# Turned aggregations of a four-layer graph network: 64x128 matmuls on two row halves of TensorE instead of 64x64 matmuls on four quadrants

## The chip, the cores and the metric

The kernel runs on one core of a Trainium2 chip. The metric is the device time of one execution in microseconds. Three runs of the kernel before gave 2742.39, 2743.45 and 2743.74 us; the median is 2743.45 us. One further execution was taken by the hardware profiler; it took 2741.53 us, and all views of the profile come from it. In those views PE is TensorE (matmuls), PEld is its weight loads, DVE is VectorE, ACT is ScalarE, POOL is GpSimd and SP is the engine that issues most transfers.

## The reference

128 graphs of 64 nodes with 512 features go through four layers. Each layer mixes the nodes of a graph with some 64x64 matrix and the features with dense weights, adds the result to its input and normalises it:

```
x = LN(x + HypergraphConv_2(LN(relu(HypergraphConv_1(x, adj))), adj) + x)   # 512 -> 1024 -> 512
x = LN(x + scaled_attention(x) @ x @ w)                                     # 64x64 matrix per graph
x = LN(x + gcn3(relu(gcn2(relu(gcn1(x))))))                                 # each: adj @ (h @ W) + b
x = LN(x + heads(softmax(q k^T) + adj + exp(-adj)) @ v @ Wout + bout)       # 8 heads of 64
```

Everything is float32. What matters here are the products of a 64x64 matrix of one graph (adj, or a matrix made from it) with that graph's 64 rows of features: `mat^T @ x`, 64x64 by 64x512.

## The kernel before

**Tiling.** Two graphs make a pair of 128 rows (128 partitions: rows 0 to 63 are one graph, rows 64 to 127 the other). Four pairs make a group of 512 rows, and 16 groups are worked through. Within a group the dense weights are applied to all 512 rows at once, and the mixing of nodes is done graph by graph.

**Dense products.** `multiply` (L546) does a 512x512 by 512x512 product with seven block products instead of eight; `product` (L528) issues the matmuls of one block product, each with a stationary operand of 128x128 and a moving one of 128x256 (L539). The first group uses plain products instead (`rows_of`, L897).

**Aggregations that come out turned.** The dense product that follows an aggregation needs its left operand with features on the partitions. So the aggregation is done with the features as the stationary operand and the graph's matrix as the moving one: the result is features by nodes, already turned. `graph_T` (L470) does this for one duo, that is two pairs or four graphs: for four chunks `c` of 128 features, two pairs `p`, two halves `f` of a chunk, and two graphs `g` of the pair, one matmul (L481) with 64 rows (the nodes of graph `g`) by 64 columns of weights (half a chunk of features) and 64 moving columns. Graph `g` sits on rows 0 to 63 or 64 to 127 of the array, half `f` on columns 0 to 63 or 64 to 127, so four matmuls in a row use the four quadrants. The results of graph `g` go to the PSUM tile `ps[g]`, whose partitions 0 to 63 and 64 to 127 are the two halves of a chunk. When the 32 matmuls are done, each of the two tiles is copied to SBUF in one instruction (ACT at L492, or DVE for the second one at L490 where `both` is set).

`graph_T` is called ten times for a group: twice for layer 0 (tiles `gt_l`, L755 or L932), four times for its hidden features (tiles `gt_l0h`, L801 or L977), twice in layer 1 (L853, or L1037 and L1064) and twice in layer 2 (L1079). `second_half` has the same loop written out for the second step of layer 2 (L1115 to L1125, tiles `gth`), where `f` and the row half `h` choose the quadrant; ACT then takes each result through a relu (L1130).

**Other small matmuls**, which stay as they are: the 64x64 matmuls on diagonal quadrants in `prepare` (`sps`, L692, and `dps`, L707, whose moving operand has one column), the attention's scores and outputs (`dot` L1326, `pv` L1385), the last aggregation of layer 2 (`agg`, L1156, 64x64 weights, 512 moving columns), and transposes with a stationary operand of 64 rows by 128 columns and 64 moving columns of an identity, on the two row halves (`xtp` L1176, `ptp` L1361).

**What orders the work.** The lists `start`, `order`, `step_1` and `step_last` (L1402 to L1422) interleave three groups: the first half of one, the second half of the group before and the tail of the one before that. The generators yield between steps, and between such points a scheduler chooses the order of each engine's instructions; `behind` (L501) holds instructions back behind a named one. PSUM has four buffers in `ps_gt` (the aggregations' results among others) and four in `ps_acc` (dense products). Weights come by DMA through a ring of 20 tiles.

Of the kernel before, what the change touches and what calls it, by code (L numbers as in the profile page):

```python
# [14 lines left out]
P = 128  # L15
C = 64
# [25 lines left out]
def kernel(  # L42
# [88 lines left out]
    ten, vec, act = Engine(nc.tensor, PE), Engine(nc.vector, DVE), Engine(nc.scalar, ACT)  # L131
# [338 lines left out]
    def graph_T(src, mat, dst, duo, key, both=False):  # L470

        ps = [ps_gt.tile([P, 4, 2, C], FP, name=f"gt_{key}_{duo}_{g}", tag="gt") for g in range(2)]
        for c in range(4):
            for p in range(2):
                for f in range(2):
                    for g in range(2):
                        rows, c0 = slice(g * C, (g + 1) * C), c * P + f * C  # L480
                        ten.matmul(  # L481
                            ps[g][f * C : (f + 1) * C, c, p, :],
                            src(2 * duo + p)[rows, c0 : c0 + C],
                            mat[rows, 2 * duo + p, :],
                            start=True, stop=True,
                        )
        o = dst[:, :, duo * Q : (duo + 1) * Q].rearrange("p c (a g i) -> p c a g i", a=2, g=2)
        for g in range(2):
            if both and g == 1:
                vec.tensor_copy(o[:, :, :, g, :], ps[g])  # L490
            else:
                act.copy(o[:, :, :, g, :], ps[g])  # L492
# [256 lines left out]
    def first_half(g):  # L749
# [4 lines left out]
        for duo in range(2):  # L754
            graph_T(pair, g["sm"], left.t, duo, f"l0_{q}")  # L755
# [42 lines left out]
        for duo in range(2):  # L798
            for u in range(2):
                with behind("l2b_0.p3") if q == 1 else nullcontext():  # L800
                    graph_T(  # L801
                        lambda p: h[p // 2][:, p % 2, u * D : (u + 1) * D], g["sm"], lefts[u].t, duo, f"l0h{u}_{q}"
                    )
            if duo == 0:
                if q == 1:
                    constant(g)
                yield "c2a"
# [43 lines left out]
        for duo in range(2):  # L851
            with behind("agg_0.p") if q == 1 else nullcontext():
                graph_T(pair, t, left.t, duo, f"l1_{q}", both=True)  # L853
# [219 lines left out]
    def second_half(g):  # L1073
# [28 lines left out]
        g2 = big.tile([P, G, D], FP, name=f"g2_{q}", tag="big")  # L1102
# [12 lines left out]
        for c2 in range(2):  # L1115
            ps = [ps_gt.tile([P, 2, G, C], FP, name=f"gth2_{q}_{c2}_{h}", tag="gt") for h in range(2)]
            for c in range(2):
                for p in range(G):
                    for f in range(2):
                        for h in range(2):  # L1120
                            rows, c0 = slice(h * C, (h + 1) * C), (2 * c2 + c) * P + f * C
                            ten.matmul(  # L1122
                                ps[h][f * C : (f + 1) * C, c, p, :],
                                g2[rows, p, c0 : c0 + C], g["atc"][rows, p, :], start=True, stop=True,
                            )  # L1125
            for c in range(2):
                k = 2 * c2 + c
                o = h2.t[:, k, :].rearrange("p (d h t) -> p d h t", d=2, h=2)
                for h in range(2):
                    act.activation(  # L1130
                        o[:, :, h, :], ps[h][:, c].rearrange("p (d a) i -> p d (a i)", d=2),
                        AF.Relu, bias=gb2_col[:, k : k + 1],
                    )
# [14 lines left out]
        for duo in range(2):  # L1148

            pool, tag = (ps_acc, "acc") if q == 0 else (ps_gt, "gt")  # L1150
            ps = [pool.tile([P, D], FP, name=f"agg_{q}_{duo}_{p}", tag=tag) for p in range(2)]
            for h in range(2):
                for p in range(2):
                    rows = slice(p * C, (p + 1) * C)
                    mat = g["atc"][rows, 2 * duo + p, :] if p == h else g["atx"][rows, duo, :]
# [13 lines left out]
        for duo in range(2):  # L1169
            ps = [ps_gt.tile([P, KD, 2, C], FP, name=f"xtp_{q}_{duo}_{h}", tag="gt") for h in range(2)]  # L1170
            for c in range(KD):
                for p in range(2):
                    for h in range(2):
                        rows = slice(h * C, (h + 1) * C)
# [39 lines left out]
        ps = attend(g, 1, pts[1], v)  # L1214
# [159 lines left out]
    def attend(g, duo, pts, v):  # L1374

        q = g["q"]

        ps = [ps_acc.tile([P, 4, 2, C], FP, name=f"pv_{q}_{duo}_{gg}", tag="acc") for gg in range(2)]
        for hc in range(4):
            for p in range(2):  # L1380
                for h2 in range(2):
                    hd = 2 * hc + h2
                    for gg in range(2):
                        rows = slice(gg * C, (gg + 1) * C)
                        ten.matmul(  # L1385
                            ps[gg][h2 * C : (h2 + 1) * C, hc, p, :],
                            v[rows, 2 * duo + p, hd * C : (hd + 1) * C],
                            pts[p][rows, h2 * 4 + hc, :],
                            start=True,
                            stop=True,  # L1390
                        )
        return ps
# [9 lines left out]
    start = """  # L1402
# [175 lines left out]
```

## Time and profile before

| what | value |
|---|---|
| runs | 2742.39, 2743.45, 2743.74 us |
| profiled execution | 2741.53 us, its span 2739.8 us |
| PE busy | 2720.2 us |
| PE weight loads busy | 2348.2 us |
| DVE busy | 2079.1 us |
| ACT busy | 804.2 us |
| POOL busy | 38.0 us |
| mean traffic of the transfers | 148 GB/s |

A span runs from the first to the last instruction; the execution holds 1.73 us more around it. A float32 matmul shows as two pairs of a weight load and a matmul, so a group's count is twice that of the code's matmuls. Each record has a start and a duration; a matmul's duration covers its way through the array, so records overlap, and the distance from one start to the next on the same part of the array tells the pace better than a duration does. In lists of groups the fields are: line, engine, operation, output and inputs by name, then for TensorE rows*columns of the weights and the shape of the operand, the count, busy time in us, mean ns of one, and the idle time before.

### The profile page before, as it was taken

Reading aid. Unit: us, or ns where it says so; the run is one execution under the profiler, and the core shown is the slowest. Engines: PE = TensorE matmul, PEld = TensorE weight load, DVE = VectorE, ACT = ScalarE, POOL = GpSimd, SP = SyncE. Lnnn points to the kernel's source line nnn. Section 1 sums busy time; section 2 is a strip of 40 time slices with the busy share of each in tenths; the row PEclk is TensorE's granted clock in tenths of the full one; section 3 lists DMA queues with packets and bytes.
Section 4 is the critical chain, followed back from the end, with each engine's and each line's share of the span. In section 5 each row is a group of like instructions: output and inputs, shape, how many; then the busy total and the mean of one; then the engine's idle time right before and its main releaser. Section 6 shows DMA issues by size and latency. Waiting matters only on the chain.

```text
span 2739.8 us, 67717 instructions
## 1 busy us (share of the span) xinstructions
PE 2720.2 (99%) x28770; PEld 2348.2 (86%) x28770; DVE 2079.1 (76%) x4119; ACT 804.2 (29%) x1442; POOL 38.0 (1%) x71
## 2 busy tenths in 40 slices
PE   9999999999999999999999999999999999999998
PEld 8878888888888888888888888888888888888887
DVE  6877687876877778787786877778777687776866
ACT  3323323232232332322223232232323323232232
POOL 2000000000000000000000000000000000000000
PEclk9999999999999999999999999999999999999999
DMA  8534454454544545445454454545545455454541
GB/s 263 180 120 153 121 174 141 141 166 131 171 132 139 166 129 169 132 143 169 132 166 130 144 164 131 166 126 153 159 131 171 130 161 146 132 164 131 151 126 60
DMA packets 309388, 405.14 MB, mean 148 GB/s; under 512 B 57408, under 2 KB 185184, under 8 KB 309088
## 3 DMA queue, kind: packets, MB, share of 16 engines
q1 hardware_dynamic: 304256, 385.58, 47.4%
q0 software_dynamic: 4832, 15.24, 1.5%
q8 instruction: 228, 3.74, 0.6%
q14 instruction: 72, 0.59, 0.1%
HBM read 369.78 MB, written 30.93 MB: 146 GB/s over the span
## 4 chain that ended last, share of the span: by engine, by line
PE 95%; DVE 3%; ACT 1%; issue 0%; DMA 0%; POOL 0%; DVEq 0%; POOLq 0%
PE a_l0w L539 15%; PE b_l0w L539 7%; PE a_l2b L539 4%; PE a_q L539 4%; PE a_k L539 4%; PE a_l2a L539 4%; PE a_v L539 4%; PE c_l0w L539 4%; PE a_l1w L539 4%; PE a_wo L539 4%; PE a_l2c L539 4%; PE gt_l L481 3%; PE gt_l0h L481 2%; PE b_l1w L539 2%; PE b_l2a L539 2%; PE b_l2b L539 2%
## 5 line engine op out<-in xcount | busy, mean ns | idle before, releaser
L539 PE MATMUL a_l0w<-w2w,aT_l0h 128*128 128x256 f32 x720 | 164.3, 381 | 0.0
L457 DVE BATCH_NORM_STATS2 st_l<-x 128x6 f32<-128x512 f32 x244 | 157.7, 673 | 0.6
L539 PEld LDWEIGHTS a_l0w<-w2w,aT_l0h 128*128 128x128 f32 x720 | 135.6, 190 | 18.8
L463 DVE TENSOR_SCALAR x<-x,mv_l,rs_l 128x512 f32<-128x512 f32 x244 | 119.3, 542 | 2.2
L539 PE MATMUL b_l0w<-w2w,s_l0h 128*128 128x256 f32 x480 | 108.5, 379 | 0.0
L779 ACT ACTIVATE h<-h 128x1024 f32<-128x1024 f32 (+1 forms) x58 | 54.9, 947 | 178.5 <-DVE h L598 157.5
L539 PEld LDWEIGHTS b_l0w<-w2w,s_l0h 128*128 128x128 f32 x480 | 91.1, 190 | 12.5
L1130 ACT ACTIVATE aT_h<-gth,gb_col 128x256 f32<-128x256 f32 x128 | 48.5, 492 | 159.0 <-PE gth L1122 159.0
L447 ACT ACTIVATE rs_l<-mv_l,eps_t 128x4 f32<-128x4 f32 (+1 forms) x64 | 19.0, 297 | 257.0 <-DVE mv_l L458 245.3
L555 DVE TENSOR_TENSOR u_l0w<-a_l0w,b_bc 128x512 f32<-128x512 f32 x56 | 38.6, 690 | 69.2 <-PE a_l0w L539 69.2
L492 ACT COPY aT_l<-gt_l 128x512 f32<-128x512 f32 x146 | 77.1, 596 | 45.7 <-PE gt_l L481 45.7
L539 PE MATMUL a_l1w<-ww,aT_l 128*128 128x256 f32 x360 | 85.7, 381 | 2.1 <-issue 2.1
L539 PE MATMUL a_l2b<-gwbw,aT_h 128*128 128x256 f32 x360 | 86.6, 383 | 0.7 <-ACT aT_oT L1397 0.7
L539 PE MATMUL a_l2c<-gwcw,aT_h 128*128 128x256 f32 x360 | 86.3, 382 | 0.0
L539 PE MATMUL a_q<-aT_xT,wqw 128*128 128x256 f32 x360 | 85.1, 379 | 0.7 <-ACT aT_xT L1181 0.7
L539 PE MATMUL a_l2a<-aT_l,gwaw 128*128 128x256 f32 x360 | 85.0, 379 | 0.0
L539 PE MATMUL a_k<-aT_xT,wkw 128*128 128x256 f32 x360 | 85.0, 379 | 0.0
L539 PE MATMUL a_l0w<-w1aw,aT_l 128*128 128x256 f32 x336 | 80.8, 383 | 0.0
L539 PE MATMUL a_v<-wvw,aT_xT 128*128 128x256 f32 x336 | 80.8, 383 | 0.0
L539 PE MATMUL a_wo<-wow,aT_oT 128*128 128x256 f32 x336 | 79.5, 379 | 0.0
L539 PE MATMUL a_l0w<-w1bw,aT_l 128*128 128x256 f32 x336 | 79.4, 379 | 0.0
L539 PEld LDWEIGHTS a_l1w<-ww,aT_l 128*128 128x128 f32 x360 | 68.5, 190 | 11.6 <-issue 2.3
(528 smaller groups left out, 6488.4 us busy)
## 6 DMA issues: line engine op xcount, KB each, us to landing
w2w<-w2k SPq DMA_DIRECT2D x210, 256.0 KB, 2.6
x<-in_x_dram SPq DMA_DIRECT2D x15, 1024.0 KB, 5.7
w1aw<-w1ak SPq DMA_DIRECT2D x60, 256.0 KB, 2.6
w1bw<-w1bk SPq DMA_DIRECT2D x60, 256.0 KB, 2.7
ww<-wk SPq DMA_DIRECT2D x60, 256.0 KB, 2.8
gwaw<-gwak SPq DMA_DIRECT2D x60, 256.0 KB, 3.1
gwbw<-gwbk SPq DMA_DIRECT2D x60, 256.0 KB, 2.7
gwcw<-gwck SPq DMA_DIRECT2D x60, 256.0 KB, 2.7
```

The source lines that it names most:

```text
L447: act.activation(rs[:, at], mv[:, at, 1], AF.Sqrt, bias=eps_t)
L457: vec.bn_stats(st, xg[:, p, :])
L463: vec.tensor_scalar(xg[:, p, :], xg[:, p, :], mv[:, p, 0:1], rs[:, p : p + 1], ALU.subtract, ALU.mult)
L481: ten.matmul(ps[g][f * C : (f + 1) * C, c, p, :], src(2 * duo + p)[rows, c0 : c0 + C], mat[rows, 2 * duo + p, :], start=True, stop=True,)
L492: act.copy(o[:, :, :, g, :], ps[g])
L539: ten.matmul(acc[:, blk, :], lhsT, rhs, start=(first and blk == 0 and i == 0), stop=(last and i == n_k - 1), skip_group_check=True,)
L555: last_add[f"{key}.{what}"] = (act.copy(t, ps) if res is None else vec.tensor_add(t, ps, res(m, n))).ins
L779: act.activation(hn, hn, AF.Relu)
L1130: act.activation(o[:, :, h, :], ps[h][:, c].rearrange("p (d a) i -> p d (a i)", d=2), AF.Relu, bias=gb2_col[:, k : k + 1],)
```

## The change

Both loops lose the index over halves of a chunk. One matmul takes the whole chunk of 128 features as its weights, so it uses 64 rows by 128 columns of the array, and the two graphs of a pair stand on the two row halves. Moving operand, PSUM tiles, their layout and the copies out of them stay. The diff is whole:

```
@@ graph_T
         for c in range(4):
             for p in range(2):
-                for f in range(2):
-                    for g in range(2):
-                        rows, c0 = slice(g * C, (g + 1) * C), c * P + f * C
-                        ten.matmul(
-                            ps[g][f * C : (f + 1) * C, c, p, :],
-                            src(2 * duo + p)[rows, c0 : c0 + C],
-                            mat[rows, 2 * duo + p, :],
-                            start=True, stop=True,
-                        )
+                for g in range(2):
+                    rows = slice(g * C, (g + 1) * C)
+                    ten.matmul(
+                        ps[g][:, c, p, :], src(2 * duo + p)[rows, c * P : (c + 1) * P],
+                        mat[rows, 2 * duo + p, :], start=True, stop=True,
+                    )
@@ second_half
             for c in range(2):
                 for p in range(G):
-                    for f in range(2):
-                        for h in range(2):
-                            rows, c0 = slice(h * C, (h + 1) * C), (2 * c2 + c) * P + f * C
-                            ten.matmul(
-                                ps[h][f * C : (f + 1) * C, c, p, :],
-                                g2[rows, p, c0 : c0 + C], g["atc"][rows, p, :], start=True, stop=True,
-                            )
+                    for h in range(2):
+                        rows, c0 = slice(h * C, (h + 1) * C), (2 * c2 + c) * P
+                        ten.matmul(
+                            ps[h][:, c, p, :], g2[rows, p, c0 : c0 + P], g["atc"][rows, p, :],
+                            start=True, stop=True,
+                        )
```

In the compiled program PE has 11825 matmuls instead of 14897: 6144 matmuls of 64x64 have become 3072 of 64x128. They stand at the same places between the same other matmuls, and no other engine has an instruction more or less.

## The prediction, made before the changed kernel ran

> **What bounds the kernel now.** I read the page from the top: busy times, the clock's row of slices, the chain that ended last.
>
> ```profile
> PE 2720.2 (99%) x28770; PEld 2348.2 (86%) x28770; DVE 2079.1 (76%) x4119; ACT 804.2 (29%) x1442; POOL 38.0 (1%) x71
> ...
> PEclk9999999999999999999999999999999999999999
> ...
> PE 95%; DVE 3%; ACT 1%; issue 0%; DMA 0%; POOL 0%; DVEq 0%; POOLq 0%
> ```
>
> TensorE is busy in 2720.2 of 2739.8 us and carries 95% of the chain; the clock is granted in full throughout. Only 19.6 us of the span are idle on PE. So what the matmuls of an aggregation take longer or shorter is given to the end nearly one to one. Next, the chain in a stretch that holds two aggregations, and the groups of TensorE by shape:
>
> ```profile
> 1146.94 2.02 PE gt_l0h L481 x128
> 1148.96 1.92 PE c_l2b L539 x8
> ```
>
> ```profile
> L481 PE MATMUL gt_l0h<-smat,h 64*64 64x64 f32 x3840 | 62.8, 220 | 0.0
> L1122 PE MATMUL gth<-atc,g 64*64 64x64 f32 x2048 | 33.8, 220 | 0.2 <-ACT g L608 0.2
> L1176 PE MATMUL xtp<-identc,x 64*128 64x64 f32 x512 | 19.9, 226 | 0.0
> ```
>
> The aggregations stand in the chain as closed blocks of 128 records between dense products: 2.02 us for 64 matmuls (two records each). Over all `gt` groups there are 10240 records, with `gth` 2048 more: 12288 records, 203 us busy, 7.4% of the span. The third line is important later: the transposes already have the shape that the change gives the aggregations (64*128 weights, 64 moving), but one record per transpose instead of two per matmul: 512 records are 16 groups of 32.
>
> **What a group of four records costs, and which part of it.** The weight loads of three blocks, in one timeline of PEld (start, time, what, count):
>
> ```profile
> 13.52 0.54 PEld L127 LDWEIGHTS dps<-atc,ht 64*64 64x64 f32 x16 [0.33 <-issue]
> ...
> 210.88 0.51 PEld L1176 LDWEIGHTS xtp<-identc,x 64*128 64x128 f32 x14 [0.33 <-issue]
> ...
> 1000.25 1.96 PEld L1122 LDWEIGHTS gth<-atc,g 64*64 64x64 f32 x128 [0.33 <-issue]
> 1002.28 0.30 PEld L539 LDWEIGHTS c_l0w<-w2w,aT_l0h 128*128 128x128 f32 x2
> ```
>
> `gth`: 128 loads on four quadrants are 32 rounds. Single starts in the trace: the four quadrants' loads start 6.7 ns apart, and a quadrant's next load comes 58.3 ns later in the steady part. 32 rounds are 1.87 us, and 0.16 us more pass before the next dense load at 1002.28 (array emptied, shape changed). So a **round costs 58.3 ns**.
>
> What sets the 58.3? `dps` tells: its weights are 64x64 too, but its moving operand has one column instead of 64. Its 16 loads on two quadrants are 8 rounds; less the last load's 0.135 us, 0.54 us make 7 distances of 58 ns; single starts say 58.3. With 64 times less to stream the pace is the same. So it is **the weight load** that sets the pace and not the streaming. The dense products give the streaming rate: 256 columns every 215.9 ns, 54.0 ns for 64 columns, just under the load's pace.
>
> The same from the first matmul after a change of shape, whose load nothing hides (min/median/max in ns):
>
> ```profile
> L539 PE MATMUL c_l0w<-w2w,aT_l0h x240: 379/379/483, 165.6 to 2520.6; 128*128 128x256 f32 x120
> ...
> L1122 PE MATMUL gth<-atc,g x2048: 218/218/267, 163.6 to 2644.7; 64*64 64x64 f32 x187
> ...
> L1176 PE MATMUL xtp<-identc,x x512: 221/223/275, 210.1 to 2673.8; 64*128 64x64 f32 x171
> ```
>
> A plain load of 64 columns adds 267 - 218 = 49 ns, one of 128 columns 483 - 379 = 104 ns. There the second load starts 55 ns after the first with 64 columns, and 106 to 108 ns after it with 128. Twice the columns, twice the load. The transposes load 128 columns in the time of 64 (275 - 223 = 52 ns; rounds of 62 ns).
>
> **The change part by part.** *Matmuls.* 12288 records in rounds of four are 3072 rounds. Now a round is two records, one on each row half, and there are again 3072. Each half loads 128 columns instead of 64 and streams the same 64. The load of 64 takes 53 ns of the 58.3 (half the 106 to 108), leaving 5 ns between; a load of 128 is 107, so a round becomes 107 + 5 = 112 ns (111.7 unrounded). That the halves load side by side is seen in `xtp`, whose two loads start 1 to 3 ns apart and share one round. Streaming 54 ns disappears behind the load. Change: 3072 x (111.7 - 58.3) = **+164 us**.
>
> The trace of before has no plain load of 64 rows by 128 columns. From below, the row of equal shape is `xtp`: 62 ns, +10 us. From above, two loads of 64 one after the other: 2 x 58.3 = 116.6 ns, +179 us; if the halves did not load side by side, 2 x 111.7 = 223 ns, +507 us. I take 111.7: the plain load of 128 columns (`c_l0w`) is the nearer row, because `xtp` goes through in another mode, one record for what a plain float32 matmul needs two for, while `c_l0w` differs only in its rows. Within that reading the bounds are 106 ns (the bare distance, +147 us) and 116.6 ns.
>
> Here two rules of the Trainium skill speak against each other. The page "TensorE: Matmul & The Clock Gate", section "LDWEIGHTS (loading the stationary operand)", says that a load's time goes by its columns and not its rows, and that a 32x128 load takes as long as a 128x128 one; that is the price of `c_l0w` for the changed kernel, and it speaks against the change. The same page, section "Wait — 56ns, not 53.3ns?", says that starts of matmuls never come closer than about 25 ns; by that a round of four would take 100 ns and one of two 50, and halving the instructions would save 3072 x 50 ns = 154 us, an estimate from that page. The trace has starts 6.7 ns apart and a round of four in 58.3 ns, so the floor does not hold across quadrants, and the measurement decides.
>
> *Changes of shape.* `gt` and `agg` share a shape today; in the first 15 groups `agg` follows straight after `gt`, without the 0.16 us. After the change it pays: 15 x 0.16 = +2.4 us. Against it, `agg` after `gt` takes 2086 ns from its first load to the next dense one, in the last group, where it stands alone, 1877: 0.21 us each is waiting for ACT and DVE to empty `gt`'s tiles, and a slower second duo gives them that time: up to 15 x 0.21 = -3.1 us. I count both together as 0, with bounds -3 and +2. The blocks' other edges change shape before and after, and stay.
>
> *Copies, adds, transfers.* ACT and DVE have the same instructions in the same order, with the same tiles. A block of two duos grows from 2.0 to 3.7 us, while the ACT copies of one duo take 2 x 0.59 us; today the blocks lose 57 ns on average over the shortest (3.7 us in all), which may vanish: 0 to -4 us. What waits for an aggregation starts later, with PE's block itself; it is covered by the dense products placed between, as today. Transfers only get more time: nothing on PE's list of idle causes is theirs in the steady part. I count 0.
>
> Sum: 2741.5 + 164 = 2905.5 us against the profiled execution. The median of the runs shown is 1.9 us over that execution; by it the same step gives 2907. I say **2906 us**.
>
> **The rivals.** (1) *Loads as in the transposes.* The 64-row shape loads 128 columns in the time that `xtp` shows. For it: same shape, same row halves. Against: two records and twice the load per column in every plain row. 3072 x (62 - 58.3) = +11 us, less up to 7 from waits: 2745 to 2753. (2) *Faster, the other side.* What the round costs today is not the load but something that goes with the number of instructions (eight in a round, 6.7 ns each, is 53 ns), and half of them leaves only the streaming: 54.0 ns, 3072 x -4.3 ns = -13 us, 2728. It decides from the point where a half loads 128 columns in less than 53 ns. Against: `dps` and `sps` have four instructions in a round and need 58.3 too. (3) *Halves load in turn*: 223 ns, +507 us, 3248. Against: `xtp`'s pairs. A lowered clock belongs here too: blocks of 3.7 us in which the array streams half of the time; the dps rows are too few to show what the clock does then. That the change does not do what it says can be excluded: the compiled order shows 64x128 matmuls, half as many, at the same places.
>
> **How the numbers follow.** Load-bound rounds 0.88, (1) 0.05, (2) 0.03, (3) or a lower clock 0.04. For the likeliest case: 106 ns, waits gone, no drain, 2741.5 + 147 - 7 = 2881; 116.6 ns and drains, 2741.5 + 179 + 2 = 2923, with the 1.9 us 2925. Those ends hold nearly all of its 0.88, so the range need not reach to the others: **2881 to 2925**. About 0.2% (5.5 us) is what a measurement here can tell from no change. Faster by more: 0.03, from (2). Within: 0.02, the lower part of (1). Slower: 0.95, the rest.
>
> **What would show it.** In the profile after: load groups of `gt` and `gth` as 64*128 64x128 with half the counts and a duration near the dense 190 ns instead of 135; blocks of 64 records with 3.7 us in the chain instead of 2.02; the first matmul of a block at about 320 ns instead of 267; `agg` near 1.9 us from its first load; idle time of PE not larger. I am wrong if the distance between a half's loads is near 62 or 54 ns (load not the bound, rivals 1 and 2), near 223 (no overlap), or if the row of the clock shows less than 9.

## The result and the profile after

The kernel after takes 2903.74 us (2903.00 to 2904.71, 4 runs), the kernel before 2742.92 us in the runs of the same chip (2742.24 to 2743.74, 4 runs). The ratio is 1.0586, with a 95% interval of 1.0573 to 1.0599: the change costs 161 us. The forecast was 2906 us in a range of 2881 to 2925. The profiled execution took 2904.18 us with a span of 2902.4, so it stands 162.6 us over that of before, in its span as well.

The page of the kernel after, in the lines that answer to those of before:

```profile
PE 2884.6 (99%) x22626; PEld 2512.9 (87%) x22626; DVE 2080.1 (72%) x4119; ACT 812.2 (28%) x1442; POOL 37.9 (1%) x71
...
PEclk9999999999999999999999999999999999999999
...
PE 98%; DVE 1%; ACT 0%; DMA 0%; issue 0%; SPq 0%
```

TensorE has 6144 records fewer and is busy 164 us longer; what is idle on it goes from 19.6 to 17.8 us. DVE's busy time is that of before; ACT's is 8 us longer, but ACT has 0% of the chain. So all of the loss is TensorE's own time. The groups by shape, and the chain in a stretch with one block:

```profile
L480 PE MATMUL gt_l0h<-smat,h 64*128 64x64 f32 x1920 | 113.7, 274 | 0.0
...
L1118 PE MATMUL gth<-atc,g 64*128 64x64 f32 x1024 | 60.7, 274 | 0.0
```

```profile
1219.30 3.72 PE gt_l0h L480 x64
1223.02 1.92 PE c_l2b L536 x8
```

Half the records, 1.8 times the busy time; a block of two duos takes 3.72 us instead of 2.02, and the dense product behind it is as long as it was (1.92). The weight loads show why:

```profile
L1118 PEld LDWEIGHTS gth<-atc,g x1024: 182/188/188, 181.6 to 2807.8; 64*128 64x128 f32 x171
L1118 PE MATMUL gth<-atc,g x1024: 272/272/320, 181.6 to 2807.8; 64*128 64x64 f32 x171
```

A load's duration is 188 ns (the dense products' 128 columns have 190). With 64 columns, in the kernel before, it was 135:

```profile
L1122 PEld LDWEIGHTS gth<-atc,g x2048: 129/135/135, 163.6 to 2644.6; 64*64 64x64 f32 x187
```

The matmul's median is 272 instead of 218, although it streams the same 64 columns: 54 ns more, as its load has 53 ns more. That the matmul's record holds the wait for the rest of its load is a reading of these two numbers; no run shows it by itself. Single starts: the two halves' loads come 6.6 ns apart, and a half's next load comes 111.7 ns later in the steady part. I added up the blocks from their first load to the first load of what follows, over the whole trace (us):

| | before | after | difference |
|---|---|---|---|
| `gt` blocks | 163.8 | 301.5 | +137.7 |
| `gth` blocks | 32.9 | 59.6 | +26.7 |
| `agg` | 33.5 | 30.6 | -2.9 |
| `xtp` | 19.4 | 19.4 | 0.0 |
| all other work of TensorE | 2485.3 | 2486.0 | +0.7 |

The sum is +162.2; another 0.5 us lies before the first load.

### The profile page after: what moved, and what is told of

It reads as the page before. It is cut to its first block, busy times and chain, and to the rows that moved or that the text cites. A ratio compares the mean times of both kernels' runs of the same rounds, so it can differ in the third digit from the quotient of the medians.

```text
span 2902.4 us, 55429 instructions
## 1 busy us (share of the span) xinstructions
PE 2884.6 (99%) x22626; PEld 2512.9 (87%) x22626; DVE 2080.1 (72%) x4119; ACT 812.2 (28%) x1442; POOL 37.9 (1%) x71
## 4 chain that ended last, share of the span: by engine, by line
PE 98%; DVE 1%; ACT 0%; DMA 0%; issue 0%; SPq 0%
PE a_l0w L536 14%; PE b_l0w L536 7%; PE gt_l L480 6%; PE a_l2b L536 4%; PE gt_l0h L480 4%; PE a_q L536 4%; PE a_k L536 4%; PE a_l2a L536 4%; PE a_v L536 4%; PE c_l0w L536 4%; PE a_l1w L536 4%; PE a_l2c L536 4%; PE a_wo L536 4%; PE pp L127 3%; PE gth L1118 2%; PE b_l1w L536 2%
## 5 line engine op out<-in xcount | busy, mean ns | idle before, releaser
L480 PEld LDWEIGHTS gt_l0h<-smat,h 64*128 64x128 f32 x1920 | 109.5, 188 | 10.0 <-issue 10.0
L480 PE MATMUL gt_l0h<-smat,h 64*128 64x64 f32 x1920 | 113.7, 274 | 0.0
L489 ACT COPY aT_l0h<-gt_l0h 128x512 f32<-128x512 f32 x120 | 64.4, 589 | 61.6 <-PE gt_l0h L480 61.6
```

Of the source, the lines that this page charges most:

```text
L480: ten.matmul(ps[g][:, c, p, :], src(2 * duo + p)[rows, c * P : (c + 1) * P], mat[rows, 2 * duo + p, :], start=True, stop=True,)
```

## The experiments

Theory: a round lasts as long as one weight load of its part of the array and 5 ns more; a load's time goes by its columns; loads of different parts run side by side; streaming lies behind the load as long as it is shorter. Rivals: load and streaming follow each other; streaming sets the pace; instructions set it; the shape and not the load is slow. Where no count of runs is given, it is one execution, the profiled one; the executions of the kernel before beside them lay between 2741.59 and 2743.80 us.

### Every second matmul streams twice as much, in the kernel after

```
-                        ps[g][:, c, p, :], src(2 * duo + p)[rows, c * P : (c + 1) * P],
-                        mat[rows, 2 * duo + p, :], start=True, stop=True,
+                        ps[g][:, c, p:, :], src(2 * duo + p)[rows, c * P : (c + 1) * P],
+                        mat[rows, 2 * duo + p : 2 * duo + 2, :], start=True, stop=True,
```

(and the same in `second_half`).

> The kernel after, but the first of every two matmuls that share weights' chunk position (even p) moves 128 columns instead of 64; the 64 too many are overwritten by the next matmul, so the result is the same. Load theory (a round is a 128-column load of 107 ns and 5 ns, the streaming lies behind it): 128 columns stream in 108 ns, still behind the load; rounds stay at 112 ns, total within 5 us of the kernel after (2904 us). Rival 'in turn' (within a row half the load takes 53 ns as in the transposes, but load and streaming follow each other, 53 + 54 + 5): half of the 3072 rounds get 54 ns longer, +83 us, 2987 us. Rival 'streaming sets it' (rounds go with the moving columns): half of the rounds double, +172 us, 3076 us.

Measured: 2901.15 us (2900.96 to 2901.28, 4 runs), 2.6 us below the kernel after; against the kernel before 1.0576 (1.0558 to 1.0594). The loads of a `gth` block in the timeline of PEld (start, from the first load to the end of the last in us, what, count, idle time before), first in this kernel:

```profile
178.42 3.65 PEld L1118 LDWEIGHTS gth<-atc,g 64*128 64x128 f32 x64 [0.33 <-issue]
```

and in the kernel after:

```profile
1244.33 3.65 PEld L1118 LDWEIGHTS gth<-atc,g 64*128 64x128 f32 x64 [0.33 <-issue]
```

Both take 3.65 us. 50% more streaming costs nothing, so neither does streaming set the pace nor does it follow the load: 53 + 54 ns in turn would have given +83 us. In a row half the next load runs while the matmul before it streams. The 2.6 us are taken up under "What was not counted", below.

### Every second matmul streams twice as much, in the kernel before

```
-                            ps[g][f * C : (f + 1) * C, c, p, :],
+                            ps[g][f * C : (f + 1) * C, c, p:, :],
...
-                            mat[rows, 2 * duo + p, :],
+                            mat[rows, 2 * duo + p : 2 * duo + 2, :],
```

(and the same in `second_half`).

> The kernel before with the same widening of every second matmul (128 moving columns, the surplus overwritten). Load theory: the quadrants' loads of 64 columns (58 ns a round) no longer cover the streaming of 108 ns; half of the 3072 rounds go from 58 to 108 to 112 ns, +76 to +82 us, 2819 to 2825 us. Rival 'in turn' (load and streaming follow each other, so a round is half load, half streaming): half of the rounds get 54 ns longer, +83 us: this run alone does not tell the two apart, the widened kernel after does. Rival 'issue sets it' (eight instructions a round): no change, 2743 us, or at most what 108 ns cost over it.

Measured: 2818.05 us, +74.8 us against the runs of before beside it (2743.27).

```profile
171.15 2.77 PEld L1122 LDWEIGHTS gth<-atc,g 64*64 64x64 f32 x128 [0.33 <-issue]
```

The same 128 loads took 1.96 us before. The time lies 1 us below the 2819 to 2825 expected; in the trace the blocks of `gt` and `gth` grew by 78.0 us. The same edit, free on two halves, costs 75 us on four quadrants, about the 76 us of half the rounds at 108 ns. Here streaming shows, because the load it could hide behind is only 53 ns. Whether eight instructions a round are what sets the 58.3 ns this run does not tell, since rounds of 108 ns would stand out over such a bound just the same. Other rows speak against it: `dps` and `sps` need 58.3 ns with four instructions a round, and the rounds of the kernel after need 111.7 with four.

### The row halves one after the other

```
-        for c in range(4):
-            for p in range(2):
-                for g in range(2):
+        for g in range(2):
+            for c in range(4):
+                for p in range(2):
```

(and `h` outermost in `second_half`).

> The kernel after with the loop over the two row halves outermost: all matmuls of the first graph of each pair, then all of the second, instead of alternating. Theory: the halves load side by side only because their instructions alternate; one after the other each record pays its own load, 112 ns, so a block of 64 matmuls takes 128 x 112 ns = 14.3 us less what... per duo 32 records x 112 ns = 3.6 us instead of 1.8; over all 6144 records 3072 x 112 ns = +343 us, about 3247 us. Rival: TensorE reaches ahead over the queue and loads the other half early; then nothing, 2904 us, or something between.

Measured: 3412.86 us, against 2743.27 of before; 509 us over the kernel after where 343 were expected. Two things differ. First, the blocks of `gt` and `gth` grew by 314 us instead of 343. Inside a half, where the clock is full, loads come 111.7 ns apart with nothing on the other half, so one load alone has that price, and it is not two halves sharing one load path. At each change of half, loads of both halves alternate for about seven records, 51 to 60 ns apart: this is the reaching ahead of the rival. It is not a small part: the five blocks that lie wholly in full clock take 6.1 us, where 64 loads one after the other would take 7.15 and the kernel after takes 3.72, so a third of the forecast growth is saved. That leaves 231 us; the other 83 of the 314 come with the clock, as the next experiment shows. Second, the dense products and `agg` behind the blocks grew by 172 and 23 us, which the expectation did not have:

```profile
604.17 7.36 PEld L480 LDWEIGHTS gt_l0h<-smat,h 64*128 64x128 f32 x64 [0.33 <-issue]
611.65 3.06 PEld L536 LDWEIGHTS c_l2b<-gwbw,aT_h 128*128 128x128 f32 x8
614.80 2.07 PEld L536 LDWEIGHTS a_l2b<-gwbw,aT_h 128*128 128x128 f32 x8
616.90 1.70 PEld L536 LDWEIGHTS b_l2b<-gwbw,s_h 128*128 128x128 f32 x8
```

The four rows are one block and the dense loads that follow it. The first eight behind the block take 3.06 us, a later eight 1.70. The profile's row of the clock shows what goes with it:

```profile
PEclk9888899899998999989898898988989999898999
```

The granted clock is 0.914 on average; in the trace it falls to half in stretches of 3.4, 6.8 or 10.2 us, 586 us in all. The stretches begin 3 to 6 us after the start of a block, while TensorE is busy (3394.6 of 3411.1 us).

### In turn, with more streaming

Added for that clock: the kernel above, and every second matmul 128 columns wide as in the first experiment.

```
-                        ps[g][:, c, p, :], src(2 * duo + p)[rows, c * P : (c + 1) * P],
-                        mat[rows, 2 * duo + p, :], start=True, stop=True,
+                        ps[g][:, c, p:, :], src(2 * duo + p)[rows, c * P : (c + 1) * P],
+                        mat[rows, 2 * duo + p : 2 * duo + 2, :], start=True, stop=True,
```

> The kernel with the two row halves in turn, and every second matmul moving 128 columns instead of 64 (the surplus is overwritten by the next matmul). It asks what made the clock fall in that kernel, where half-clock stretches took 586 us and the dense products 172 us more. Theory (the clock falls because too little of the array streams for too long: one half streams 54 of every 112 ns): the blocks stay as long, since 128 columns stream behind the load, but the array streams 1.5 times as much, so there is less half-clock time and the total lies below 3413 us, at the least about 3220 us if no half-clock stretch is left. Rival (the clock follows the number of matmuls or loads in a time, not what they stream): same half-clock time, 3413 us.

Measured: 3134.35 us (before beside it 2741.59), 279 us less than without the surplus work. Blocks and clock:

```profile
203.07 6.04 PEld L1118 LDWEIGHTS gth<-atc,g 64*128 64x128 f32 x64 [0.33 <-issue]
209.18 3.32 PEld L536 LDWEIGHTS c_l0w<-w2w,aT_l0h 128*128 128x128 f32 x16
```

```profile
PEclk9999999999999999999999999999999999999999
```

No half-clock stretch is left but the start and the end; `agg` is back at 30.3 us, the other work at 2485.6. The time lies even below the 3220 that I had called the least, because that number kept the blocks at the length they had in the trace above, where the half clock had stretched them too: without it all blocks together take 592 us instead of 675. Against the 361 us of the kernel after, the halves in turn therefore cost 231 us at full clock; the lowered clock adds 83 us in the blocks and 195 in the work behind them. So in this pair of runs it is the amount streamed that decides over the clock; the matmuls and loads are as many in both, in the same order.

### The second loop alone

Only the hunk of `second_half` of the change, in the kernel before.

> The kernel before with only the second loop changed (gth, the hidden step of layer 2): 512 of the 3072 rounds. Theory: 512 x 53.4 ns = +27 us, 2770 us, the gth blocks at 3.72 us instead of 2.03 and the gt blocks unchanged; the rest of the kernel gives nothing back. Rival: part of the longer block is hidden or paid elsewhere (the relus of ACT behind it, waits before the next dense product): less or more than 27 us.

Measured: 2770.80 us, +27.5 us.

```profile
164.19 3.65 PEld L1121 LDWEIGHTS gth<-atc,g 64*128 64x128 f32 x64 [0.33 <-issue]
167.91 0.73 PEld L539 LDWEIGHTS c_l0w<-w2w,aT_l0h 128*128 128x128 f32 x4
```

The `gth` blocks add up to 59.6 us as in the kernel after; the `gt` blocks, which were not changed, have 166.0, 2.2 us more than before. Of these, 2.0 us are one block at 2291.9 us in which TensorE stands for 1.9 us; an instruction transfer of 16 KB begins 0.5 us before that and ends 0.5 us after its start. A sixth of the rounds brings a sixth of the loss; in sum the rest of the kernel gives nothing back.

### The transposes as plain matmuls

```
-                            ten.transpose(
-                                ps[h][:, c, p, :], xg[rows, 2 * duo + p, c * P : (c + 1) * P], identc[rows]
-                            )
+                            ten.matmul(
+                                ps[h][:, c, p, :], xg[rows, 2 * duo + p, c * P : (c + 1) * P], identc[rows],
+                                start=True, stop=True,
+                            )
```

> The kernel before with the 512 transposes of L1176 (64x128 weights, 64 moving columns of an identity, row halves alternating) as plain float32 matmuls of the same operands. Theory (their 62 ns a round come from the mode of the transpose and not from the shape): 1024 records in 512 rounds of 112 ns, 57 us instead of 256 x 62 ns = 16 us: +41 us, 2784 us. Rival (the shape loads 128 columns in 62 ns whatever the mode): 512 x 62 ns, +16 us, 2759 us.

Measured: 2781.49 us, +39.2 us against 2742.32 beside it.

```profile
L1176 PEld LDWEIGHTS xtp<-identc,x x1024: 182/188/188, 210.1 to 2714.1; 64*128 64x128 f32 x171
L1176 PE MATMUL xtp<-identc,x x1024: 272/272/320, 210.1 to 2714.1; 64*128 64x64 f32 x171
```

The transposes' loads in the kernel before:

```profile
L1176 PEld LDWEIGHTS xtp<-identc,x x512: 134/139/143, 210.0 to 2673.7; 64*128 64x128 f32 x171
```

Same operands, same shape, same places: twice the records, a load of 188 ns instead of 139, and the pace of the aggregations after the change (111.7 ns). The `xtp` blocks go from 19.4 to 59.6 us. The 62 ns belong to the transpose's mode.

### Eight parts of 64x32

```
-                for f in range(2):
+                for f in range(4):
                     for g in range(2):
-                        rows, c0 = slice(g * C, (g + 1) * C), c * P + f * C
+                        rows, c0 = slice(g * C, (g + 1) * C), c * P + f * 32
...
-                            ps[g][f * C : (f + 1) * C, c, p, :],
-                            src(2 * duo + p)[rows, c0 : c0 + C],
+                            ps[g][f * 32 : (f + 1) * 32, c, p, :],
+                            src(2 * duo + p)[rows, c0 : c0 + 32],
```

(in both loops; then, as a second kernel, in `second_half` alone).

> The opposite step to the change: chunks of 32 features, 64 rows x 32 columns of weights, eight matmuls a round on eight parts of the array in both loops. Load theory: a load of 32 columns is 27 ns and falls behind the streaming of 64 columns, so a round costs 54 to 58 ns, as the eight pairs of instructions at 6.7 ns each (54 ns) also allow: 0 to -13 us, 2730 to 2743 us. Rival 'issue': each of the 16 instructions takes its own 6.7 ns, 107 ns a round, +150 us, 2893 us. Rival 'fixed floor': the round costs 58 ns for any number of columns up to 64, 2743 us exactly.

Measured: 3105.33 us (3094.64 to 3107.19, 4 runs), ratio 1.1324 (1.1306 to 1.1343). No expectation fits. The distances of a part's loads in the first `gth` block are 40, 43, 56, 56, 195, 66, 67, 67, 111, ... ns, then one of 1956. The first rounds stay within the 55 ns or so that the load theory allows; later ones do not.

> The kernel before with 64x32 weights on eight parts in the gth loop alone (512 of the 3072 rounds). With both loops so cut the kernel took 3105 us; its first rounds took 55 ns as the load theory has it, later ones 67 to 112 ns, and single stops of 2 to 3.6 us stood in the blocks. Theory (TensorE runs out of instructions: the stops are fetches that come too late when blocks follow one another too closely): with a sixth of the blocks cut, the rounds still slow down to some 78 ns, 2.66 us a block instead of 2.03, +10 us, but the long stops are gone, 2753 us. Rival (the stops belong to the 32-column form itself): 16 blocks at 5.1 us as in the kernel with all loops cut, +50 us, 2792 us.

Measured: 2801.68 us, +60.1 us against 2741.59. The rival holds: the stops stay where only a sixth of the blocks is cut. The `gth` blocks take 81.4 us instead of 32.9; 11 us more lie in the other work, in a run with 32 us at half clock. One block in PEld's timeline:

```profile
163.79 1.77 PEld L1122 LDWEIGHTS gth<-atc,g 64*32 64x32 f32 x171 [0.33 <-issue]
168.04 0.91 PEld L1122 LDWEIGHTS gth<-atc,g 64*32 64x32 f32 x85 [2.47 <-issue]
```

Within the block TensorE stands for 2.47 us, and the profile names nothing it waits for ("issue"). Fourteen of the sixteen `gth` blocks have such a stop, and in all fourteen an instruction transfer of 16 KB (queue q8 of the profile) starts between 0.3 us before the stop and 1.0 us into it, and has landed 1.2 to 1.5 us before the next load starts. That TensorE waits for these instructions is likely from the order of times; it was not tried by itself.

## Why the prediction was right

**The bound.** "What the matmuls of an aggregation take longer or shorter is given to the end nearly one to one": blocks +164.4 us, the span +162.6.

**What sets the 58.3 ns.** I read it off `dps`, whose single moving column had the same pace. The two widened kernels show the same from the other side: streaming is free while it is shorter than the load, and costs its full excess where it is not.

**The size.** 3072 x (111.7 - 58.3) = 164.0 us were forecast, the blocks give 164.4, at a steady 111.7 ns. The bounds of 106 and 116.6 were wider than needed. The mechanism is right; that the sums agree within 0.4 us is in part luck. A steady block grew by 1.69 us (2.025 to 3.718) where the sum has 1.71; the first block, at half clock, grew by 3.6; and one at 195.2 us did not grow at all, because it had 2.26 us of idle time at its end before, and 0.56 after. The choice between the nearest rows, `c_l0w` for its plain mode against `xtp` for its equal shape, carried the forecast, and the plain transposes show that it was right for the reason given. The first matmul of a block was to take about 320 ns; it takes 320.

**Changes of shape.** The trace has 14 groups in which `agg` follows straight after `gt`, not 15. From `gt`'s last load to `agg`'s first it is 256 ns instead of 38, +0.22 us each and not 0.16. `agg` fell from 2086 to 1902 ns, not to 1877. The two cancel (+3.0 and -2.9 us), as counted.

**What was not counted.** The start. The prediction read a clock "granted in full throughout" from the page's row of tenths. The trace of before has it in full from 9.6 us on, with one stretch of 3.41 us at half from 200.7 us. The first block meets the array at half clock (timelines of PE; kernel before, kernel after, widened kernel after):

```profile
6.35 3.59 PE L127 MATMUL gt_l<-smat,x 64*64 64x64 f32 x128 [0.45 <-ACT smat L127]
9.87 3.72 PE L127 MATMUL pp<-w1ab,aT_l 128*128 128x256 f32 x16
```

```profile
6.84 7.19 PE L127 MATMUL gt_l<-smat,x 64*128 64x64 f32 x64 [0.45 <-ACT smat L127]
13.96 6.04 PE L127 MATMUL pp<-w1ab,aT_l 128*128 128x256 f32 x16
```

```profile
6.84 6.33 PE L127 MATMUL gt_l<-smat,x 64*128 64x128 f32 x64 [0.45 <-ACT smat L127]
13.09 3.72 PE L127 MATMUL pp<-w1ab,aT_l 128*128 128x256 f32 x16
```

The full clock comes at 18.7 us in the kernel after, so its first sixteen dense records take 6.04 us instead of 3.72. The widened kernel after has it at 12.1; at the first transposes it is 3.2 us ahead (225.4 against 228.6 us), which covers the 2.6 us it gained. That more streaming in that block brings the clock earlier is not shown: of the two kernels with the halves in turn, the one that streams more has it later (23.6 against 21.6 us).

Against the start stands what the kernel before lost around 200 us. Its idle time there (the block at 195.2 us above) was followed by the 3.41 us at half clock, and the dense products behind it took 1.1 us longer than in the kernel after, which has no such stretch. With smaller stalls this is the 0 to -4 us that the prediction let vanish, and it makes up for about as much as the start cost: the sum ended 1.3 us below the 2905.5 forecast for the profiled execution.

**The rivals.** (1) falls with the plain transposes, (2) with the blocks of 3.72 us, (3) with the halves in turn, which show what the missing overlap would have cost. Its second half, the lowered clock, did not come in this change, but for the longer start; it is there when the same streaming is spread over blocks of 6 us and more instead of 3.7.

In this case a rule of the Trainium skill that the prediction used held with a number that the trace of before lacked: the page "TensorE: Matmul & The Clock Gate", section "LDWEIGHTS (loading the stationary operand)", has a load's time go by its columns and not by its rows, and here 64 rows by 128 columns take 188 ns in the profile as 128 by 128 take 190. The 25 ns between starts of its section "Wait — 56ns, not 53.3ns?" do not show across quadrants (6.7 ns) nor across halves (6.6 ns).

## What to carry to other kernels

Where the weights of a matmul are used for one short moving operand, count the columns that each part of the array has to load, not the matmuls: with 64 moving float32 columns a round with 64 columns of weights took 58 ns (on two parts and on four) and one with 128 took 112 (on one part and on two). So here the cut to take was the one with load and streaming about equally long (53 and 54 ns); merging parts into wider ones halved the instructions and nearly doubled the time of a round, and the one finer cut was slower too, for a reason that was not settled. Find out which of the two bounds by looking for a group with the same weights and another moving length, and for the first matmul after a change of shape, which shows its load uncovered; and let matmuls of different parts alternate.

## What the runs showed of the hardware that was not expected

- The granted clock fell to half while TensorE was busy without a gap: blocks in which one row half at a time streamed 54 of every 112 ns brought 586 us at half clock, some 195 us in other work and 83 us in the blocks themselves; with 1.5 times the streaming and the same instructions the clock stayed full. In the kernel after, with both halves at 54 of 112 ns, it stayed full too. Elsewhere a half-clock stretch came after idle time of TensorE: each of the eight of 3.41 us in the run with 64x32 in `second_half` alone begins 0.8 to 1.5 us after the end of an idle stretch of 2.1 to 3.3 us.
- Eight parts of 64x32 ran at 55 ns a round for a few rounds, and then mostly at 67 to 112 ns. With 64x32 in `second_half` alone, 14 of 16 blocks had a stop of 2 to 3.4 us, each with an instruction transfer of 16 KB at it. The traces of the kernels before and after have no such stop in their blocks; a single one, of 1.9 us, stands in a four-quadrant block of the run with the second loop alone. A version that beats both kernels did not come out of these runs: between 58.3 ns and the 54 ns of streaming only about 13 us are to be had (3072 x 4.3 ns, an estimate), and the one finer cut that was tried takes 363 us more than the kernel before.
